# A four-layer graph network on one core: the hand-ordered slots of the attention layer replaced by a greedy assignment of tiles and steps to engines

## The chip, the cores and the metric

The kernel runs on one core of a Trainium2 chip. The core has a matrix engine (TensorE, PE), three engines for elementwise work (VectorE or DVE, ScalarE or ACT, GpSimd or POOL) and queues for transfers (here SyncE or SP issues most of them). Each engine executes its own instructions in program order and waits on semaphores for the others. Results of PE land in PSUM, of which the kernel uses eight banks of 128 x 512 float32; GpSimd works on SBUF alone in this kernel, the others on both. The metric is the device time of one execution in microseconds.

## The reference

Input x has 64 batches of 256 nodes with 128 features, and there is one 256 x 256 adjacency matrix. Four layers follow, each behind a layer norm with a ReLU and with a residual sum. All is float32. Cut to what matters:

```python
# layer 0: five steps of a gated graph network (both matrices are adj)
m = einsum('nm,bmd->bnd', adj, h);  av = concat([m, m])
z = sigmoid(av @ w3.T + w3_b + h @ u3.T + u3_b)
r = sigmoid(av @ w4.T + w4_b + h @ u3.T + u3_b)
hv = tanh(av @ w5.T + w5_b + (r * h) @ u5.T + u5_b)
h = (1 - z) * h + z * hv
# layer 1: Chebyshev hops with adj, a product with Theta1, bias, ReLU
# layer 2: (adj @ h + h) @ weight + bias, each row scaled to norm 1
# layer 3: attention over pairs of nodes (i, j), with 256 features e
pre = s1[:, :, None, :] + s2[:, None, :, :] + b_lin   # s1, s2: products of h and adj
hh  = where(pre >= 0, pre, 0.2 * pre)
e   = einsum('bije,e->bij', hh, a) + adj
out = sigmoid(einsum('bij,bjf->bif', softmax(e, axis=2), h))
x   = x + out
```

The costly part is layer 3: for each batch, 256 x 256 pairs of nodes times 256 features go through a leaky ReLU and a weighted sum over the features.

## The kernel before

**Pairs, slots and tiles.** Two batches are handled together, which makes 32 pairs. The leaky ReLU is split into a linear part, which is one projection with `g2` into the score bank, and 0.8 times a ReLU. The ReLU part is built tile by tile: a tile is 128 features x (4 rows i, 2 batches, 256 nodes j), 128 x 2048 values. A pair has 64 slots, numbered n over the whole kernel, with 4 rows i in each, and each slot has two tiles, k = 0 and k = 1, for the two halves of the 256 features. So there are 2048 slots and 4096 tiles. `scores` (L637 to L650) multiplies each tile with a window of the weight vector (`win`), four matmuls side by side, which add into the score bank of its block. A block is 32 slots, half a pair; the two score banks are used in turn.

**Who makes tiles.** `make` (L611 to L635) lets DVE make the k = 0 tile of each slot with one tensor_tensor, max(s2a, -s1 - b), from the PSUM bank `s2a`, which holds s2 of this pair and is written by one projection at the first slot of the pair (`"t_2a" not in ops`). The part that this leaves out of the ReLU is linear in i alone and cancels in the softmax over j. For k = 1 there are two kinds: in two slots of three (kind "g") GpSimd adds s1 and s2 in `make_sum` (L602 to L608, seven slots ahead) and ACT applies the ReLU to the whole tile in place (L625); in the third (kind "s") ACT makes the tile alone with eight activations of 256 values, with s1 as the bias and s2 read from a PSUM bank `s2p` (L635). Each kind has its own buffers: five for k = 0, six and two for k = 1, thirteen in all.

**Fronts and tails.** What comes before the scores of a pair p (layers 0 to 2 and the projections of layer 3) is a generator `front(p)`; its last act is to put its operands into `READY[p]`. What comes after a block (softmax, the product with h3, output) is `tail(p, ic, ...)`. A generator yields, before each step, the engine of this step, the time from which it can run, and whether it needs a spare PSUM bank; four of the eight banks are spare. A step is one to a few instructions. `norm`, `copied`, `project_token`, `to_feature` and others are helpers of these generators; where a helper issues an instruction, its line stands in the profile (L259 is that of all side-by-side matmuls but the scores).

**Order.** The program order is written while the kernel is traced. The code keeps a clock for each engine (`ran`, with a price for each step and a delay `SEEN` until others see it), and `in_order` pins each engine's instructions in the order of tracing. Fronts 0 and 1 are begun first, and front 0 is completed before the first slot. Then for each slot n: `background(n)` advances fronts and tails whose step can run by the clocks, or that are behind a due time; then the sum of slot n + 7, the tiles of slot n + 4, and the scores of slot n are issued. Front p + 2 begins when pair p's first slot comes, so two fronts are under way at once, each over about two pairs.

Of the kernel before, what the change touches and what calls it, by code (L numbers as in the profile page):

```python
# [21 lines left out]
AHEAD = 4  # L22
SUM_AHEAD = 7
# [4 lines left out]
def kernel(  # L28
# [50 lines left out]

# [12 lines left out]
    s2a, s2p = (b.rearrange("p (b n) -> p b n", b=NB) for b in banks[:2])  # L92
    pes = banks[2:4]
# [3 lines left out]
    SEEN = {PE: 0.25, DVE: 0.14, ACT: 0.15, POOL: 0.13}  # L97

    def ran(engine, us, *after):
        clock[engine] = max(clock[engine], 0.0, *after) + us  # L100
        return clock[engine] + SEEN[engine]

    spare = [[b, 0.0] for b in banks[4:]]
# [6 lines left out]
    def by_feature(b):  # L110
        return b.rearrange("p (b n) -> p b n", b=NB)
# [123 lines left out]
    nc.vector.memset(win, 0.0)  # L235
    a_rep = const.tile([P, NE, P], F32, name="a_rep")
    nc.vector.memset(a_rep, 1.0)
    nblin = const.tile([P, NE], F32, name="nblin")
    nc.vector.tensor_scalar(nblin, blin, -1.0, None, op0=OP.mult)
    for k in range(NE):  # L240
        nc.vector.tensor_scalar(win[:, k, 31:32], acol[:, k:k + 1], 1.0 - ALPHA, None, op0=OP.mult)
        nc.vector.tensor_scalar(a_rep[:, k, :], a_rep[:, k, :], acol[:, k:k + 1], None, op0=OP.mult)
# [46 lines left out]
    def project_token(pp, pairs):  # L289

        pp = by_token(pp)
        for b in range(NB):
            for c in range(NC):
                for k, (t, w) in enumerate(pairs):
                    nc.tensor.matmul(pp[:, b, c, :], t[:, b, c * P:(c + 1) * P], w,  # L295
                                     start=(k == 0), stop=(k == len(pairs) - 1))
# [13 lines left out]
    PROJECT, MIX, TURN, PRODUCT, PRODUCTS = 0.86, 1.74, 0.69, 1.18, 2.99  # L310
    COPY, BIASED, TANH, ELEMENTS = 0.48, 0.58, 0.57, 0.61

    def norm(src, since, h):
# [9 lines left out]
        t = ran(DVE, 1.04, since)  # L323
        yield POOL, t
        inverse_root(mv[:, :, 1], OP.add, LN_EPS)
        nc.gpsimd.tensor_scalar(mv[:, :, 0], mv[:, :, 0], -1.0, None, op0=OP.mult)
        nc.gpsimd.tensor_mul(mv[:, :, 0], mv[:, :, 0], mv[:, :, 1])  # L327
        t = ran(POOL, 1.6, t)
# [13 lines left out]
    KEPT = {"hT": dict(bufs=4), "hT3": {}, "s2b": {}}  # L342
# [3 lines left out]
    def front(p):  # L346
# [144 lines left out]
        yield DVE, t  # L491
# [15 lines left out]
        hT, t_hT = copied("hT3", b, t)  # L507
        yield PE, t_hT, 1
        b = take()
        project(b[0], adj_t[:, 1, P:2 * P], hT)  # L510
        t = ran(PE, PROJECT, t_hT, b[1])
        yield ACT, t
        s2b, t_2 = copied("s2b", b, t)
# [14 lines left out]
        s1n = feat("s1n")  # L528
        nc.scalar.activation(s1n, by_feature(b[0]), AF.Identity, bias=nblin[:, 0:1], scale=-1.0)
        t_n = ran(ACT, BIASED, t)  # L530
        spare.append([b[0], t_n])
        READY[p] = dict(x3=x3, h3=h3, hT=hT, s1n=s1n, s1b=s1b, s2b=s2b, t_b=max(t_b, t_2), t_n=t_n)

    def tail(p, ic, pe, since, x3, h3):
# [27 lines left out]
        for k in range(NB):  # L562
            for c in range(NC):
                nc.tensor.matmul(po[:, k, :], wT[:, k, c, :], h3[:, k, c, :], start=(c == 0), stop=(c == NC - 1))  # L564
# [19 lines left out]
    TILES = {}  # L584
    t_pe = {}
    t_free = {"v": [0.0] * 5, "g": [0.0] * 6, "s": [0.0] * 2}
# [5 lines left out]
    def kind(n):  # L592
        return "s" if n % 3 == 0 else "g"

    def operands(n, s1, s2):

        _, ic, r = where(n)
        i0 = ic * P + r
        whole = [P, 4, NB, N]
        rows = s1[:, :, i0:i0 + 97:32].rearrange("p b g -> p g b").unsqueeze(3)  # L600
        return s2.unsqueeze(1).to_broadcast(whole), rows.to_broadcast(whole)

    def make_sum(n):
        if n >= NPAIR * SLOTS or kind(n) != "g":
            return
        ops = READY[where(n)[0]]
        tile_ = relu_pool.tile([P, 4, NB, N], F32, name="rl_g", bufs=6)
        nc.gpsimd.tensor_add(tile_, *operands(n, ops["s1b"], ops["s2b"]))  # L608
        TILES[n, 1] = tile_, ran(POOL, 3.58, ops["t_b"], t_free["g"].pop(0))

    def make(n):  # L611
        if n >= NPAIR * SLOTS:
            return
        p, ic, r = where(n)
        ops = READY[p]
        if "t_2a" not in ops:
            project(banks[0], adj_t[:, 1, 0:P], ops["hT"])
            ops["t_2a"] = ran(PE, PROJECT, clock[DVE] + SEEN[DVE])
        tile_ = relu_pool.tile([P, 4, NB, N], F32, name="rl_v", bufs=5)
        nc.vector.tensor_tensor(tile_, *operands(n, ops["s1n"], s2a), op=OP.max)  # L620
        TILES[n, 0] = tile_, ran(DVE, 2.2, ops["t_2a"], ops["t_n"], t_free["v"].pop(0))
        if kind(n) == "g":
            tile_, since = TILES[n, 1]
            t = tile_.rearrange("p g b n -> p (g b n)")
            nc.scalar.activation(t, t, AF.Relu)  # L625
            TILES[n, 1] = tile_, ran(ACT, 1.8, since)
        else:
            if "t_2p" not in ops:
                nc.scalar.copy(s2p, ops["s2b"])
                ops["t_2p"] = ran(ACT, COPY, ops["t_b"])  # L630
            tile_ = relu_pool.tile([P, 4, NB, N], F32, name="rl_s", bufs=2)
            for g in range(4):
                for b in range(NB):
                    i = ic * P + g * 32 + r
                    nc.scalar.activation(tile_[:, g, b, :], s2p[:, b, :], AF.Relu,  # L635
                                         bias=ops["s1b"][:, b, i:i + 1], scale=1.0)
            TILES[n, 1] = tile_, ran(ACT, 2.86, t_free["s"].pop(0))  # L637

    def scores(n):
        p, ic, r = where(n)  # L640
        pe = pes[ic % 2]
        if r == 0:
            project(pe, g2, READY[p]["hT"], stop=False)
            ran(PE, PROJECT, t_pe.get(p * NC + ic - 2, 0.0))
        for k in range(NE):
            tile_, since = TILES.pop((n, k))

            for g in range(4):
                nc.tensor.matmul(pe[g * 32:(g + 1) * 32, :], win[:, k, 31 - r:63 - r], flat(tile_[:, g]),  # L649
                                 start=False, stop=(r == 31 and k == NE - 1), skip_group_check=True)  # L650
            t_free["v" if k == 0 else kind(n)].append(ran(PE, PROJECT, since))

    CHAINS = {}

# [3 lines left out]
    def begin_front(p):  # L658
        if p < NPAIR:
            load_x(p + 1)  # L660
            begin(p, front(p))

    def wait_of(key):

        engine, since, *bank = CHAINS[key][1]
        if bank:
            if not spare:
                return 1e9
            since = max(since, min(b[1] for b in spare))
        return since - clock[engine]  # L670

    def advance(key):
        chain = CHAINS[key]
        chain[1] = next(chain[0], None)
        chain[2] += 1
        if chain[1] is None:
            del CHAINS[key]
        return chain[2]

    in_order()  # L680
    for e in clock:
        clock[e] = 0.0
    begin_front(0)
    begin_front(1)
    total = 0
    while 0 in CHAINS:

        q = 1 if 1 in CHAINS and wait_of(1) < wait_of(0) - 1.0 else 0
        taken = advance(q)
        total = taken if q == 0 else total  # L690
        in_order()

    def background(n):
        p, k = n // SLOTS, n % SLOTS + 1
        room = SLOTS - SUM_AHEAD - 3
        while True:
            todo = []
            for key in CHAINS:
                if isinstance(key, tuple):
                    late = 2.0  # L700
                else:

                    due = total * (0.5 * (min(1.0, k / room) + 1) if key == p + 1 else 0.5 * k / SLOTS)
                    late = due - CHAINS[key][2]
                todo.append((-late, key))
            for late, key in sorted(todo, key=lambda x: x[0]):
                late = -late
                if late < -AHEAD_STEPS:
                    continue
                wait = wait_of(key)  # L710
                if wait <= TOLERANCE or late > LATE and wait < 100 or key == p + 1 and k >= room:
                    break
            else:
                return
            advance(key)

    AHEAD_STEPS, TOLERANCE, LATE = 15, 0.05, 8

    for n in range(SUM_AHEAD):
        make_sum(n)  # L720
    for n in range(AHEAD):
        make(n)
    in_order()
    for n in range(NPAIR * SLOTS):
        if n % SLOTS == 0:
            begin_front(n // SLOTS + 2)
        background(n)
        make_sum(n + SUM_AHEAD)
        make(n + AHEAD)
        scores(n)  # L730
        in_order()
        if n % 32 == 31:
            p, ic, _ = where(n)
            begin((p, ic), tail(p, ic, pes[ic % 2], clock[PE] + SEEN[PE], READY[p]["x3"], READY[p]["h3"]))
    while CHAINS:
        advance(min(CHAINS, key=wait_of))
# [31 lines left out]
```

## Time and profile before

| What | Value |
|---|---|
| Runs | 5560.47, 5561.85, 5564.78 us; median 5561.85 |
| The profiled execution's own time | 5561.99 us |
| Its span, first to last instruction | 5560.2 us |
| Mean granted TensorE clock | 0.989 |
| First DVE tile | at 146.87 us |
| HBM traffic | 9.70 MB read, 8.39 MB written, 3 GB/s over the span |

The time of a run and the span differ by 1.8 us, which lie outside the first and last instruction. Busy time is the union of an engine's instructions; instructions that overlap on one engine have durations whose sum is larger than the busy time, so what an instruction occupies is better read from the distance between two starts. Idle time is put down to what ended it. The transfers are small beside the span and stay out of the following.

### The profile page before, as it was taken

How to read it: one execution, taken by the hardware profiler on the slowest of the kernel's cores; microseconds unless marked ns; L12 is line 12 of the kernel's file. 1: busy time of each engine (PE TensorE's matmuls, PEld its weight loads, DVE VectorE, ACT ScalarE, POOL GpSimd, SP SyncE). 2: the span in 40 equal slices, each digit the busy share in tenths (PEclk: the TensorE clock that was granted, in tenths of full speed). 3: DMA queues.
4: the chain of work that ended last, by engine and by line, in shares of the span. 5: the costliest groups of instructions: out<-in, count | busy, mean ns of one | idle time of the engine just before them, and what ended most of it. 6: DMA issues, size and time to landing. Idle time of an engine off the chain costs nothing.

```text
span 5560.2 us, 122022 instructions
## 1 busy us (share of the span) xinstructions
PE 5364.9 (96%) x51733; PEld 1876.4 (34%) x51733; DVE 5273.8 (95%) x4224; ACT 5390.2 (97%) x8910; POOL 5222.9 (94%) x2075
## 2 busy tenths in 40 slices
PE   7999999999999999999999999999999999999998
PEld 3333333333333333333333333333333333333322
DVE  3989999999999999999999999999999999999998
ACT  3999999999999999999999999999999999999998
POOL 1999999999999999999999999999999999999998
PEclk9999999999999999999999999999999999999999
DMA  0000000000000000000000000000000000000000
GB/s 20 2 4 5 5 2 5 5 4 5 4 3 5 4 5 5 2 5 5 4 5 4 3 5 4 5 5 2 5 5 4 5 4 3 5 2 3 3 2 4
DMA packets 38741, 25.91 MB, mean 5 GB/s; under 512 B 3504, under 2 KB 38192, under 8 KB 38192
## 3 DMA queue, kind: packets, MB, share of 16 engines
q1 hardware_dynamic: 35088, 17.05, 1.0%
q8 instruction: 404, 6.62, 0.5%
q10 hardware_dynamic: 3104, 1.05, 0.1%
q14 instruction: 145, 1.19, 0.1%
HBM read 9.70 MB, written 8.39 MB: 3 GB/s over the span
## 4 chain that ended last, share of the span: by engine, by line
PE 56%; DVE 20%; ACT 16%; issue 6%; POOL 2%; DMA 0%; ACTq 0%; DVEq 0%; POOLq 0%; SPq 0%
PE bank L649 35%; DVE rl_v L620 16%; PE bank L259 16%; ACT rl_g L625 7%; ACT rl_s L635 6%; POOL rl_g L608 2%; PE bank L295 2%; PE bank L287 2%; PE bank L564 1%; ACT h L331 1%; DVE bank L404 1%; PE bank L280 1%; DVE d L400 1%; DVE hT L408 1%; DVE stats L320 0%
## 5 line engine op out<-in xcount | busy, mean ns | idle before, releaser
L608 POOL TENSOR_TENSOR rl_g<-s2b,s1b 128x2048 f32<-128x2048 f32 x1365 | 4901.1, 3626 | 147.6 <-PE bank L649 133.5
L620 DVE TENSOR_TENSOR rl_v<-bank,s1n 128x2048 f32<-128x2048 f32 x2048 | 4576.9, 2280 | 151.9 <-PE bank L649 89.8
L625 ACT ACTIVATE rl_g<-rl_g 128x2048 f32<-128x2048 f32 x1365 | 2846.3, 2198 | 19.0 <-POOL rl_g L608 18.7
L635 ACT ACTIVATE rl_s<-bank,s1b 128x256 f32<-128x256 f32 x5464 | 2226.4, 730 | 41.2 <-PE bank L649 40.1
L649 PE MATMUL bank<-rl_v,win 128*32 128x512 f32 x16384 | 2187.9, 599 | 12.0 <-DVE rl_v L620 11.6
L649 PE MATMUL bank<-rl_g,win 128*32 128x512 f32 x10920 | 1434.4, 595 | 14.3 <-ACT rl_g L625 14.3
L649 PEld LDWEIGHTS bank<-rl_v,win 128*32 128x32 f32 x16384 | 514.1, 110 | 1068.2 <-issue 933.2
L649 PE MATMUL bank<-rl_s,win 128*32 128x512 f32 x5464 | 754.5, 595 | 0.5 <-ACT rl_s L635 0.5
L649 PEld LDWEIGHTS bank<-rl_g,win 128*32 128x32 f32 x10920 | 352.5, 111 | 858.4 <-issue 710.6
L649 PEld LDWEIGHTS bank<-rl_s,win 128*32 128x32 f32 x5464 | 190.2, 110 | 439.5 <-issue 374.2
L259 PE MATMUL bank<-adj_t,h 128*32 128x256 f32 x5120 | 309.5, 382 | 7.4 <-ACT h L419 7.4
L259 PE MATMUL bank<-hT,adj_t 128*32 128x512 f32 x1024 | 149.0, 662 | 105.4 <-DVE rl_v L620 104.6
L259 PEld LDWEIGHTS bank<-adj_t,h 128*32 128x32 f32 x5120 | 156.2, 110 | 156.0 <-ACT h L419 34.8
L331 ACT ACTIVATE h<-x,mv 128x128 f32<-128x128 f32 x384 | 166.5, 581 | 11.8 <-POOL mv L327 11.7
L259 PE MATMUL bank<-mT,w 128*32 128x512 f32 x1280 | 168.3, 592 | 0.0
L259 PE MATMUL bank<-mT,w5t 128*32 128x512 f32 x1280 | 168.3, 592 | 0.0
L259 PE MATMUL bank<-rh,u5t 128*32 128x512 f32 x1280 | 168.2, 592 | 0.0
L395 ACT ACTIVATE bank<-bank,gate_b 128x512 f32<-128x512 f32 x160 | 156.5, 978 | 11.6 <-PE bank L259 11.2
L259 PE MATMUL bank<-hT,u3t 128*32 128x512 f32 x1280 | 166.7, 593 | 0.0
L259 PE MATMUL bank<-mT,w4t 128*32 128x512 f32 x1280 | 166.7, 592 | 0.0
L377 ACT ACTIVATE bank<-bank,gate_b 128x512 f32<-128x512 f32 x160 | 152.1, 951 | 13.2 <-PE bank L259 13.0
L381 DVE SCALAR_TENSOR_TENSOR rh<-bank,hT 128x512 f32<-128x512 f32 x160 | 109.3, 683 | 56.7 <-ACT bank L377 55.7
(111 smaller groups left out, 3458.7 us busy)
## 6 DMA issues: line engine op xcount, KB each, us to landing
xin<-in_x_dram SPq DMA_DIRECT2D x64, 128.0 KB, 2.2
out_dram<-o SPq DMA_DIRECT2D x64, 128.0 KB, 1.8
w_raw<-in_L_gnn_w_w_dram ACTq DMA_DIRECT2D x3, 128.0 KB, 2.6
th_raw<-in_L_gnn_Theta_dram ACTq DMA_DIRECT2D x1, 320.0 KB, 3.3
adj_n<-in_adj_dram SPq DMA_DIRECT2D x1, 256.0 KB, 5.0
w_raw<-in_L_gnn_u_w_dram ACTq DMA_DIRECT2D x2, 64.0 KB, 2.2
bias<-in_L_gnn_bias_dram ACTq DMA_DIRECT2D x2, 64.0 KB, 3.4
w<-in_L_gnn_weight_dram ACTq DMA_DIRECT2D x1, 64.0 KB, 3.0
```

Source lines behind the costliest of these rows:

```text
L259: nc.tensor.matmul(o[g:g + 32], w[:, g:g + 32], t, start=start, stop=stop, skip_group_check=True)
L287: nc.tensor.transpose(pt[:, b, c, :], ht[:, b, c * P:(c + 1) * P], ident)
L295: nc.tensor.matmul(pp[:, b, c, :], t[:, b, c * P:(c + 1) * P], w, start=(k == 0), stop=(k == len(pairs) - 1))
L331: nc.scalar.activation(h[:, k, :], s[:, k, :], AF.Relu, bias=mv[:, k, 0:1], scale=mv[:, k, 1:2])
L377: nc.scalar.activation(r[0], pr[0], AF.Tanh, bias=br, scale=0.5)
L381: nc.vector.scalar_tensor_tensor(rh, by_feature(r[0]), 1.0, hT, op0=OP.add, op1=OP.mult)
L395: nc.scalar.activation(pv[0], pv[0], AF.Tanh, bias=bh, scale=1.0)
L608: nc.gpsimd.tensor_add(tile_, *operands(n, ops["s1b"], ops["s2b"]))
L620: nc.vector.tensor_tensor(tile_, *operands(n, ops["s1n"], s2a), op=OP.max)
L625: nc.scalar.activation(t, t, AF.Relu)
L635: nc.scalar.activation(tile_[:, g, b, :], s2p[:, b, :], AF.Relu, bias=ops["s1b"][:, b, i:i + 1], scale=1.0)
L649: nc.tensor.matmul(pe[g * 32:(g + 1) * 32, :], win[:, k, 31 - r:63 - r], flat(tile_[:, g]), start=False, stop=(r == 31 and k == NE - 1), s ...
```

## The change

The slots are gone as an order. Names and code that change:

- Each engine takes work for itself. The main loop picks the engine whose simulated time is lowest; of the work that is ready for it (tail steps first, then front steps, then a tile) it issues one item, else it moves that engine's time on.
- DVE takes the k = 0 tiles in order, one instruction each; ACT and GpSimd share the k = 1 tiles, each taking the next when it comes free. ACT makes a tile in two parts of four activations, GpSimd in four parts of two `tensor_scalar` instructions of 256 values with a per-partition scalar. The pass of ACT over GpSimd's sums is gone.
- Signs: s2 is projected negated (`w2n`), DVE and GpSimd take the minimum and not the maximum, and their tiles meet the negated window `win_n`; ACT uses scale = -1.0.
- The thirteen tile buffers are one set; an engine holds at most 8 (DVE), 3 (ACT) or 2 (GpSimd) that are not yet scored.
- PE scores whichever tile was ready first; a block's end is counted with `left`.
- The bank of s2 for DVE is doubled (`s2v`, by the parity of the pair) and is written by a step of the front. Score banks and `s2p` move on by one, and three banks are spare in place of four.
- A front begins when `2 + scored // 128` exceeds the number begun; its steps are held back by a due time. A step of the front (x3) waits until the tail of the pair two before it has been issued.
- `project_token` and the product in `tail` use four column groups (`side_by_side`) in place of one 128-wide matmul.
- In `norm` the sign change of the mean moves from GpSimd to DVE. Prices in the planner change too.

The diff, cut to its core:

```diff
-    s2a, s2p = (b.rearrange("p (b n) -> p b n", b=NB) for b in banks[:2])
-    pes = banks[2:4]
+    s2v = banks[:2]
+    s2p = banks[2].rearrange("p (b n) -> p b n", b=NB)
+    pes = banks[3:5]
-    SEEN = {PE: 0.25, DVE: 0.14, ACT: 0.15, POOL: 0.13}
+    SEEN = {PE: 0.25, DVE: 0.14, ACT: 0.45, POOL: 0.13}
-    spare = [[b, 0.0] for b in banks[4:]]
+    spare = [[b, 0.0] for b in banks[5:]]
...
-                    nc.tensor.matmul(pp[:, b, c, :], t[:, b, c * P:(c + 1) * P], w,
-                                     start=(k == 0), stop=(k == len(pairs) - 1))
+                    side_by_side(pp[:, b, c, :], t[:, b, c * P:(c + 1) * P], w, k == 0, k == len(pairs) - 1)
...
-    PROJECT, MIX, TURN, PRODUCT, PRODUCTS = 0.86, 1.74, 0.69, 1.18, 2.99
+    PROJECT, MIX, TURN, PRODUCT, PRODUCTS = 0.86, 1.74, 0.69, 0.88, 2.64
...
+        nc.vector.tensor_scalar(mv[:, :, 0], mv[:, :, 0], -1.0, None, op0=OP.mult)
...
-        nc.gpsimd.tensor_scalar(mv[:, :, 0], mv[:, :, 0], -1.0, None, op0=OP.mult)
...
-        yield DVE, t
+        yield DVE, t, 0, lambda: p < 2 or (p - 2, NC - 1) in TAILED
         x3 = tok("x3")
...
+        s2a = s2v[p % 2]
+        yield PE, max(t_hT, t_s2v[p % 2])
+        project(s2a, w2n[:, 0:P], hT)
+        t_s2a = ran(PE, PROJECT, t_hT, t_s2v[p % 2])
...
+    tiles = [[relu_pool.tile([P, 4, NB, N], F32, name=f"rl{k}", bufs=1), 0.0] for k in range(13)]
+    MOST = {DVE: 8, ACT: 3, POOL: 2}
...
+    def tile_ready(e):
+        if e in begun:
+            return 0.0
+        n = following[e != DVE]
+        if n >= NSLOT or n // SLOTS not in READY or held[e] == MOST[e] or not tiles:
+            return None
+        return max(READY[n // SLOTS]["since"][e != DVE], min(t[1] for t in tiles))
...
+    def work_on_tile(e):
...
+        if e == DVE:
...
+            nc.vector.tensor_tensor(t, rows.to_broadcast(whole), ops["s2a"].unsqueeze(1).to_broadcast(whole), op=OP.min)
+            done = ran(DVE, 2.2, since)
...
+        elif e == ACT:
...
+            for g in (2 * part, 2 * part + 1):
+                for b in range(NB):
+                    i = i0 + g * 32
+                    nc.scalar.activation(t[:, g, b, :], s2p[:, b, :], AF.Relu, bias=ops["s1"][1][:, b, i:i + 1], scale=-1.0)
+            done = ran(ACT, 1.43, since)
         else:
...
+            for b in range(NB):
+                i = i0 + part * 32
+                nc.gpsimd.tensor_scalar(t[:, part, b, :], ops["s2n"][:, b, :], ops["s1"][1][:, b, i:i + 1], None, op0=OP.min)
+            done = ran(POOL, 1.8, since)
...
+    def score_ready():
+        best = None
+        for tile_ in made:
...
+            if block not in left:
+                if block >= 2 and block - 2 not in t_pe:
+                    continue
+                since = max(since, t_pe.get(block - 2, 0.0))
+            if best is None or since < best[0]:
+                best = since, tile_
+        return best
...
+    STEPS_OF_FRONT, SPREAD, AHEAD = 106, 1.8, 8
...
+    def chain_ready(key, e):
...
+        if not isinstance(key, tuple) and key > 0:
+            due = STEPS_OF_FRONT * (scored[0] / (2 * SLOTS) - (key - 2)) / SPREAD
+            if CHAINS[key][2] > due + AHEAD:
+                return None
+        return max(since, min(b[1] for b in spare)) if bank else since
...
+    while scored[0] < 2 * NSLOT or CHAINS:
+        while begun_fronts[0] < NPAIR and begun_fronts[0] < 2 + scored[0] // (2 * SLOTS):
+            begin_front()
+        e = min(now, key=now.get)
...
+        ready = [x for x in todo if x[0] <= now[e] + 0.05]
+        if ready:
+            _, (rank, *_), what = min(ready, key=lambda x: x[1])
+            if rank < 2:
+                advance(what)
+            elif e == PE:
+                score(what)
             else:
+                work_on_tile(e)
```

## The prediction, made before the changed kernel ran

> **What bounds the kernel now.** I read the page's first two parts, then busy time by stretch, then the waits and groups, and last the timeline for what one instruction really occupies.
>
> ```profile
> PE 5364.9 (96%) x51733; PEld 1876.4 (34%) x51733; DVE 5273.8 (95%) x4224; ACT 5390.2 (97%) x8910; POOL 5222.9 (94%) x2075
> ...
> DVE  3989999999999999999999999999999999999998
> ```
>
> Four engines are over 94% busy, so none alone can be called the bound. The leading 3 of DVE is the prologue: the first tile starts at 146.87 us. Then the stretches:
>
> ```profile
> 2000.00:2169.00 169.00, 164.42 (x1608) 57.53 (x1604) 163.76 (x132) 168.07 (x280) 162.90 (x65) 0.99 0.02 5
> 2169.00:2338.00 169.00, 165.74 (x1616) 58.20 (x1612) 163.94 (x132) 167.36 (x277) 162.49 (x66) 0.99 0.02 4
> ```
>
> The columns are PE, PEld, DVE, ACT, POOL. One pair of batches takes about 169 us. The starts of the copy on L629, which comes once per pair, are 146.40 us for pair 0 and 5397.87 us for pair 31: 5251.5 / 31 = 169.4 us a pair. The periods go 167, 167, 174.5 and again. DVE has 164.2 us of work in it; ACT is busy for nearly all of it. Where the rest goes:
>
> ```profile
> POOL rl_g L608 <- PE bank L649: 133.5, 71, 4.5
> ...
> PE bank L259 <- DVE rl_v L620: 104.6, 31, 4.5
> ...
> DVE rl_v L620 <- PE bank L649: 89.8, 87, 2.6
> ...
> DVE rl_v L620 <- PE bank L259: 59.1, 31, 10.9
> ```
>
> (total us, times, longest.) The lines with 31 are the pair boundaries: PE stands 3.4 us before the product into s2a because DVE still reads the old one, and DVE then waits 1.9 us for that product. The L649 lines are makers that wait for a tile buffer.
>
> ```profile
> L608 POOL TENSOR_TENSOR rl_g<-s2b,s1b 128x2048 f32<-128x2048 f32 x1365 | 4901.1, 3626 | 147.6 <-PE bank L649 133.5
> L620 DVE TENSOR_TENSOR rl_v<-bank,s1n 128x2048 f32<-128x2048 f32 x2048 | 4576.9, 2280 | 151.9 <-PE bank L649 89.8
> L625 ACT ACTIVATE rl_g<-rl_g 128x2048 f32<-128x2048 f32 x1365 | 2846.3, 2198 | 19.0 <-POOL rl_g L608 18.7
> L635 ACT ACTIVATE rl_s<-bank,s1b 128x256 f32<-128x256 f32 x5464 | 2226.4, 730 | 41.2 <-PE bank L649 40.1
> ```
>
> These durations overlap, so the timeline gives the occupancy:
>
> ```profile
> 2004.47 3.68 ACT L635 ACTIVATE rl_s<-bank,s1b 128x256 f32<-128x256 f32 x8
> 2007.32 2.63 ACT L625 ACTIVATE rl_g<-rl_g 128x2048 f32<-128x2048 f32 x1
> 2009.12 1.38 ACT L392 ACTIVATE bank<-bank,gate_b 128x512 f32<-128x512 f32 x1
> ```
>
> Start to start, eight short activations take 2.85 us, one Relu pass 1.80, a tanh 0.57. The same reading gives 2.20 us for a DVE tile and 0.86 for a tile on PE.
>
> **What the Trainium skill says.** "TensorEngine Tiling (Array Packing)", Key Properties: a change of tiling mode drains the TensorE. The trace agrees: the 128-wide product on L295 starts 0.11 us late between 32-wide ones and holds PE for 1.20 us where its eight matmuls are 0.11 apart. "TensorE: Matmul & The Clock Gate", "Wait — 56ns, not 53.3ns?": start to start is never under about 25 ns; here 32 matmuls of 256 columns take 1.73 us, 54 ns each, so 128 columns would come at 27, just above. "GPSIMD Engine Reference", Engine selection: two-input operations pay for a shared read port, one-input ones run near line rate. The trace: 738 ns for a two-input 128x256 (L578), 408 for a one-input (L577). "SBUF — State Buffer", Who interferes with whom: a DVE instruction with at most one SBUF input leaves GpSimd alone; the DVE tile reads one operand from PSUM before and after. No run here tests that.
>
> **The change, part by part.**
>
> DVE: still makes all 2048 tiles of k = 0, min in place of max, 64 x 2.20 = 141 us a pair, plus the same steps. The sign change in norm comes over from POOL: 4 x 0.08 = 0.3 us a pair. 164.2 + 0.3 = 164.5. This is the new floor, since DVE is given no k = 1 tile.
>
> ACT and POOL: the 1365 Relu passes (1365 x 1.80 = 2457 us) go, and both engines now make whole k = 1 tiles. ACT's other work is 31 us a pair (5390 - 2457 - 683 x 2.85 = 986 us, / 32). An ACT tile costs 2.85. A POOL tile is eight tensor_scalar with a per-partition scalar, 128x256, which the trace doesn't show. From below: 8 x 0.49 (L577 with its gap) = 3.9 us. From above: like the two-input L578 with a gap, 8 x 0.83 = 6.6, or the planner's 8 x 0.90 = 7.2 in the diff. The planner's other prices agree with the trace within 0.1 us a step, so I take 7.2. Then at 167 us a pair ACT can make (167 - 31) / 2.85 = 48 tiles and POOL (167 - 9) / 7.2 = 22: 70 for the 64 needed. 6 tiles of slack; both fall behind DVE as limits. If one instruction really takes over 0.955 us, the 21 tiles that the plan puts there take 21 x 7.64 + 9 = 169.5 us and POOL gives all back.
>
> PE: the same tiles. From spacings, a pair is 159 units of 0.86 (tiles, projections), 8 node mixes of 1.73, 10 transposes of 0.69 and the 128-wide products (3.0 + 1.2 + 2 x 1.2): 136.7 + 13.8 + 6.9 + 6.6 = 164.0. The products in four column groups at 27 ns cost 2.64 + 3 x 0.88 = 5.3: 1.3 us less, 162.7. If 54 ns were a floor for them they would cost 10.4 and PE 167.8.
>
> s2 in two banks: the boundary waits (3.4 us of PE, 1.9 of DVE a pair) go. Price: three spare banks in place of four. A front holds two (pr and r or pv), a tail one: enough for one front at a time. Tiles in any order, 13 shared buffers: PE no longer stands behind a late tile, and the 174.5 us periods, which come from the n % 3 pattern, go too.
>
> Fronts: before, two fronts run at once, each over two pairs. Now front q begins when 128 (q - 1) tiles are scored, so it has about one pair's time to become READY. Its latency is the new question. In the prologue front 0 takes from its first stats at 23.98 us to 146.87: 122.9 us, front 1 beside it. Adding its steps by the spacings gives 118, so 119 alone. Under load each step that comes from another engine waits for the rest of a tile piece: DVE 19 steps x 0.86 busy x 1.1 = 18 us, and three norms that come 0.14 us after a DVE step and so behind a whole tile, 3 x 2.06 less their share, +3; ACT 33 x 0.76 x 0.71 = 18; PE 32 x 0.64 x 0.43 = 9; POOL 5 x 0.9 x 0.9 = 4. Together 52 us, less 1 for the sign change: L = 170 us.
>
> **The sum.** With L above a pair's work W, front q + 1 begins when pair q - 1 is used up, which is before READY[q]: the stall is g = L - P and the period P = (L + W) / 2. W = 164.5 + 1 to fill PE = 165.5. In the stall the chain runs unhindered, so L = 170 - 0.3 g. This gives g = 2.0, P = 167.5. Time = 146.9 prologue (the two first fronts as before) + 31 x 167.5 + 157 for the last pair (no front left: 64 x 2.2 + 4 of tails, then 11 us from last score to end as now) + 1.8 outside the span = 5498 us. Against the profiled run's 5561.99 (span 5560.2) and the median of the runs, 5561.85, 1.1% less. I take 5495.
>
> **The rivals.**
> 1. The front fits into the pair (L under 165): DVE never stalls, P = 165.5, time 5436. For it: the k = 1 makers may run ahead of DVE, which brings `scored` and so the next front forward. Against: my waits add up to more. Chance 0.20.
> 2. The front is late: one chain with about 105 hand-overs on loaded engines replaces two overlapping ones. Where the waits are 70 us and not 52, L = 187, g = 9.5, P = 175, time 5730. It decides from L = 174, where P = 169.5 as now. For it: three spare banks, and DVE tiles slip in wherever a step is ready 0.14 us later. Against: steps go ahead of tiles on every engine. Chance 0.20.
> 3. POOL's instruction is dearer than 0.955 us: at 1.05, 21 x 8.4 + 9 = 185 us a pair, about 6050. Against: both measured neighbours are under 0.83. Chance 0.08.
> 4. Nothing much is left: engines at 98% in a fixed order slip on small differences between plan and chip, or small matmuls cost PE 54 ns: P = 168.5 to 170, 5530 to 5576. For it: two periods in three are already 167. Chance 0.10.
>
> **Numbers.** My forecast, 5460 to 5540, has 0.42; the rivals as above. The range 5420 to 5650 leaves out rival 3, the far half of 2 and little else. What this kernel's measurement can tell from no change is about 0.2%, 11 us. Faster: 0.40 + 0.20 + 0.04 = 0.64; same 0.06; slower 0.30.
>
> **What would show it.** The L259 boundary waits gone from the waits; no Relu over whole tiles, about 43 ACT tiles and 21 POOL tiles a pair; DVE 97 to 98% busy from 150 us on; one DVE idle of about 2 us a pair, ended by ACT's s1a or the s2 copy (rival 2: over 6 us a pair there; rival 1: none). POOL's tensor_scalar near 0.9 us; over 0.955 with PE waiting for POOL is rival 3. L295 and L564 in fours 0.11 us apart. I am wrong in the mechanism if DVE's idle is behind PE or POOL and not at READY.

## The result, and the profile after

| | Before | After |
|---|---|---|
| Median of four runs | 5561.84 us (5560.47 to 5564.78) | 5522.43 us (5521.90 to 5525.01) |
| Span of the profiled execution | 5560.2 us | 5520.6 us |

The ratio is 0.9929, with a 95% interval from 0.9912 to 0.9947: the changed kernel is 0.7% faster. The forecast was 5495 us, 1.2% faster, in a range from 5420 to 5650.

First lines of parts 1 and 2 of the changed kernel's page. Then the busy time by stretch (PE, PEld, DVE, ACT, POOL, each with its number of instructions, then clock and DMA): one stretch in the kernel before, then the same in the changed one.

```profile
PE 5376.7 (97%) x56341; PEld 1942.7 (35%) x56341; DVE 5314.8 (96%) x4355; ACT 5012.2 (91%) x13193; POOL 5038.5 (91%) x5854
...
ACT  3998899989989998999899899989998999999898
```

```profile
1000.00:2000.00 1000.00, 978.51 (x9592) 344.41 (x9588) 971.61 (x778) 991.50 (x1646) 962.49 (x385) 0.99 0.02 5
```

```profile
1000.00:2000.00 1000.00, 984.18 (x10444) 351.48 (x10440) 981.75 (x803) 924.43 (x2438) 934.79 (x1086) 1.00 0.02 5
```

ACT went from 991 us in 1000 to 924 and POOL from 962 to 935; DVE rose from 972 to 982 and PE from 979 to 984. So ACT and POOL have slack now, and DVE and PE are nearly full. Which of the two bounds the kernel, if either does, these shares don't tell. The costly groups of the page show that the makers do what the diff says:

```profile
L647 POOL TENSOR_SCALAR rl<-s2n,s1b 128x256 f32<-128x256 f32 x5272 | 4741.5, 937 | 103.5 <-PE bank L685 51.8
L628 DVE TENSOR_TENSOR rl<-s1a,bank 128x2048 f32<-128x2048 f32 x2048 | 4552.1, 2278 | 39.6 <-ACT s1a L534 39.6
L641 ACT ACTIVATE rl<-bank,s1b 128x256 f32<-128x256 f32 x11112 | 4436.2, 978 | 1.0
```

No Relu over whole tiles is left. GpSimd makes 5272 / 8 = 659 tiles (20.6 a pair), ACT 11112 / 8 = 1389 (43.4 a pair). A GpSimd tile costs 4741.5 / 659 = 7.19 us.

What DVE waits for, over the whole span (total us, times, longest):

```profile
DVE d L400 <- ACT bank L395: 50.1, 31, 5.1
DVE rl L628 <- ACT s1a L534: 39.6, 21, 10.3
DVE rs L573 <- ACT sc L552: 29.9, 11, 2.9
DVE rh L381 <- ACT bank L377: 21.5, 24, 9.9
```

The waits of DVE's tiles for L259 (now L260) and for buffers behind L649 (now L685) are gone from this list. In their place stands the wait of a tile for `s1a`, the last thing that a front makes. Most of `d` and `rh` falls into the first 400 us, as the same list from 400 to 5200 us shows:

```profile
DVE rs L573 <- ACT sc L552: 28.8, 10, 2.9
DVE rl L628 <- ACT s1a L534: 26.5, 19, 2.8
DVE d L400 <- ACT bank L395: 8.0, 18, 0.5
DVE rh L381 <- ACT bank L377: 6.0, 19, 0.5
```

Two pair boundaries of DVE's timeline show what the first two lines are:

```profile
2148.45 4.47 DVE L628 TENSOR_TENSOR rl<-s1a,bank 128x2048 f32<-128x2048 f32 x2
2152.84 0.86 DVE L320 BATCH_NORM_STATS2 stats<-xin 128x6 f32<-128x128 f32 x4
...
2154.91 0.69 DVE L547 TENSOR_REDUCE nmx<-sc 128x2 f32<-128x512 f32 x1
2158.47 0.17 DVE L573 RECIPROCAL rs<-sums 128x2 f32<-128x2 f32 x1 [2.87 <-ACT sc L552]
2161.40 6.68 DVE L628 TENSOR_TENSOR rl<-s1a,bank 128x2048 f32<-128x2048 f32 x3 [2.76 <-ACT s1a L534]
...
2310.31 17.66 DVE L628 TENSOR_TENSOR rl<-s1a,bank 128x2048 f32<-128x2048 f32 x8
2327.90 0.68 DVE L543 TENSOR_TENSOR sc<-bank,adj_n 128x512 f32<-128x512 f32 x1
```

At 2152.84 the tiles of one pair have run out. Until 2161.40 DVE has only some steps, and it idles 2.87 + 2.76 = 5.6 us, although the first of these idles carries the name of another step. ACT's timeline has `s1a` at that moment, and the columns at its end say that ACT was waiting for PE's projection:

```profile
2160.68 0.69 ACT L534 ACTIVATE s1a<-bank,blin 128x512 f32<-128x512 f32 x1 [0.23 <-PE bank L260]
```

At the next boundary tiles run through from 2310.31 to 2327.97, with no gap. At the one after that DVE idles for 0.2 us, and then the pattern begins again. The starts of `s1a` come every 163.1, 170.8 and 172.6 us and again; from 468.63 us (pair 2) to 5362.71 (pair 31) the mean is 4894.08 / 29 = 168.8 us, against 169.4 before. The first statistics of a front come right behind the used-up pair, and from there to its `s1a` are 165.4 us (809.73 to 975.10), 174.7 (972.97 to 1147.69) and 171.0 (1139.85 to 1310.83), and so on in this pattern: 170.4 on average. So a front takes about as long as a pair, and now and then DVE stands waiting for it. That this is what keeps the gain small is the reading which the experiments test.

### The profile page after: what moved, and what is told of

It is laid out like the page before. It is cut to its first block, busy times and chain, and to the rows that moved or that the text cites. A ratio compares the mean times of both kernels' runs of the same rounds, so it can differ in the third digit from the quotient of the medians.

```text
span 5520.6 us, 138813 instructions
## 1 busy us (share of the span) xinstructions
PE 5376.7 (97%) x56341; PEld 1942.7 (35%) x56341; DVE 5314.8 (96%) x4355; ACT 5012.2 (91%) x13193; POOL 5038.5 (91%) x5854
## 4 chain that ended last, share of the span: by engine, by line
PE 46%; DVE 28%; ACT 22%; issue 3%; POOL 1%; DMA 0%; ACTq 0%; POOLq 0%; SPq 0%; DVEq 0%
PE bank L685 29%; DVE rl L628 22%; ACT rl L641 17%; PE bank L260 15%; PE bank L288 1%; ACT bank L395 1%; DVE stats L320 1%; DVE bank L404 1%; ACT h L331 1%; DVE hT L408 1%; ACT bank L377 1%; DVE d L400 1%; ACT h L419 1%; PE bank L281 1%; ACT sc L552 1%
## 5 line engine op out<-in xcount | busy, mean ns | idle before, releaser
L647 POOL TENSOR_SCALAR rl<-s2n,s1b 128x256 f32<-128x256 f32 x5272 | 4741.5, 937 | 103.5 <-PE bank L685 51.8
L628 DVE TENSOR_TENSOR rl<-s1a,bank 128x2048 f32<-128x2048 f32 x2048 | 4552.1, 2278 | 39.6 <-ACT s1a L534 39.6
L641 ACT ACTIVATE rl<-bank,s1b 128x256 f32<-128x256 f32 x11112 | 4436.2, 978 | 1.0
L685 PE MATMUL bank<-rl,win_n 128*32 128x512 f32 x21656 | 2785.3, 594 | 29.7 <-DVE rl L628 28.4
L685 PE MATMUL bank<-rl,win 128*32 128x512 f32 x11112 | 1598.2, 594 | 0.0
L685 PEld LDWEIGHTS bank<-rl,win_n 128*32 128x32 f32 x21656 | 734.4, 110 | 1487.9 <-issue 1196.7
L685 PEld LDWEIGHTS bank<-rl,win 128*32 128x32 f32 x11112 | 397.0, 110 | 766.7 <-issue 567.0
L260 PE MATMUL bank<-adj_t,h 128*32 128x256 f32 x5120 | 318.1, 382 | 17.0 <-ACT h L419 16.4
L260 PEld LDWEIGHTS bank<-adj_t,h 128*32 128x32 f32 x5120 | 166.5, 110 | 199.1 <-ACT h L419 89.5
L377 ACT ACTIVATE bank<-bank,gate_b 128x512 f32<-128x512 f32 x160 | 172.7, 1079 | 58.8 <-issue 29.1
L392 ACT ACTIVATE bank<-bank,gate_b 128x512 f32<-128x512 f32 x160 | 176.7, 1105 | 8.9 <-PE bank L260 8.9
L395 ACT ACTIVATE bank<-bank,gate_b 128x512 f32<-128x512 f32 x160 | 170.9, 1068 | 14.3 <-PE bank L260 14.3
L337 ACT COPY mT<-bank 128x512 f32<-128x512 f32 x160 | 165.6, 1035 | 15.7 <-PE bank L260 15.6
L260 PE MATMUL bank<-hT,u3t 128*32 128x512 f32 x1280 | 175.3, 594 | 0.0
L260 PE MATMUL bank<-mT,w4t 128*32 128x512 f32 x1280 | 174.6, 594 | 0.0
L260 PE MATMUL bank<-mT,w 128*32 128x512 f32 x1280 | 174.1, 592 | 0.0
L260 PE MATMUL bank<-rh,u5t 128*32 128x512 f32 x1280 | 174.0, 592 | 0.0
L260 PE MATMUL bank<-mT,w5t 128*32 128x512 f32 x1280 | 174.0, 592 | 0.0
L419 ACT COPY h<-bank 128x512 f32<-128x512 f32 x128 | 149.1, 1165 | 5.1 <-PE bank L288 5.1
```

Source lines behind the costliest of these rows:

```text
L260: nc.tensor.matmul(o[g:g + 32], w[:, g:g + 32], t, start=start, stop=stop, skip_group_check=True)
L337: nc.scalar.copy(c, by_feature(bank[0]))
L377: nc.scalar.activation(r[0], pr[0], AF.Tanh, bias=br, scale=0.5)
L392: nc.scalar.activation(pr[0], pr[0], AF.Tanh, bias=bz, scale=0.5)
L395: nc.scalar.activation(pv[0], pv[0], AF.Tanh, bias=bh, scale=1.0)
L419: nc.scalar.copy(h, by_token(b[0]))
```

## The experiments

Each ratio is to the kernel before, measured beside the run on the same chip (5562.9 to 5566.3 us there, 5561.8 beside the changed kernel). So a difference between a run and the changed kernel's 5522.43 us is uncertain by some 4 us. The names: theory F is that of the front's latency, P = (L + W) / 2 for a period P (from one pair to the next), a latency L (from a front's first statistics to its `s1a`) and a pair's work W on DVE; D says that DVE's work is the bound, E that PE's is.

### Fronts begun earlier

```diff
-        while begun_fronts[0] < NPAIR and begun_fronts[0] < 2 + scored[0] // (2 * SLOTS):
+        while begun_fronts[0] < NPAIR and begun_fronts[0] < 2 + (scored[0] + SLOTS) // (2 * SLOTS):
```

> Each front begins 64 tiles, half a pair, earlier than in the changed kernel; nothing else is touched. Theory F (the front's latency of 165 to 175 us against a pair's work sets the period, P = (L + W) / 2): a front that has half a pair more is READY in time, the stall before s1a goes, and the period falls from 168.8 us to DVE's own work plus small waits, 166 to 167.5: 5430 to 5480 us. Rival D (DVE, 98% busy, is the bound and its idle is slip between plan and chip) and rival E (PE, 96% full by its spacings, is the bound): the period stays, 5505 to 5535 us.

5437.53 us, ratio 0.9769 [0.9753, 0.9786]: 85 us less than the changed kernel, by one added term, as F said. D and E, under which nothing should have changed, don't hold for the changed kernel. The same stretch of this run, and the next:

```profile
1000.00:2000.00 1000.00, 989.94 (x10612) 351.08 (x10608) 996.48 (x804) 944.98 (x2492) 955.53 (x1112) 1.00 0.02 5
2000.00:3000.00 1000.00, 990.09 (x10655) 352.45 (x10651) 996.59 (x822) 943.78 (x2489) 950.91 (x1109) 1.00 0.02 5
```

DVE is 99.65% busy, and its wait list between 2000 and 5190 us is empty, where the changed kernel has 44 us. The starts of `s1a` come every 165.6 us (1083.74 to 2574.13, nine periods). Two fronts are under way at once for a part of the time, and each takes longer: 194.1 us from 392.05 to 586.15. They are ready in time all the same. No kernel of the study is faster.

### Fronts begun later

```diff
+        while begun_fronts[0] < NPAIR and begun_fronts[0] < 2 + max(0, scored[0] - 8) // (2 * SLOTS):
```

> Each front begins 8 tiles, about 10 us, later than in the changed kernel. Theory F: the front of pair q + 1 now begins after READY of pair q, so the period is its latency plus this delay, 12 + 170 us less what the idle engines save: 175 to 180 us, 5720 to 5880 us. Rivals D and E: a chain that is ready some us later in a schedule that has other work changes nothing: under 5550 us.

5813.21 us, ratio 1.0444 [1.0429, 1.0460], with periods of 179.4, 178.5 and 178.0 us, as F said. Of its DVE waits:

```profile
DVE rl L628 <- ACT s1a L534: 332.3, 31, 11.7
```

The wait comes once for every pair boundary, 10.7 us each. Ten microseconds of a single chain's start cost 290 us, 9.4 a pair: at the boundary DVE has no other tile to make. A front takes a little less here than in the changed kernel: 166.3, 167.7 and 166.8 us (845.54 to 1011.79, 1023.51 to 1191.22, 1202.94 to 1369.69).

### Inner norms that follow at once

Behind x1, x2 and x3 the time handed to `norm` is DVE's own clock, without the 0.14 us until others see the result. One of the three places:

```diff
         t = ran(DVE, ELEMENTS, t)
         spare.append([b[0], t])
+        t = clock[DVE]
```

> The statistics of the three inner norms may follow the DVE step before them at once, where in the changed kernel they are ready 0.14 us later and stand behind a whole tile of 2.20 us. No instruction is added or taken away. Theory F: L falls by 3 x 2.06 = 6 us, the period by up to 3 us: 5430 to 5490 us. Rivals D and E: the engines' work is the same, 5505 to 5535 us.

5459.27 us, ratio 0.9810 [0.9796, 0.9825]. No instruction less, and 63 us are gone, as F said. From the first statistics to `s1a` it is now 162.4 and 164.8 us (1133.70 to 1296.11, 1303.39 to 1468.23), 170.4 before: 6.8 us less, for 6 that were expected. By the formula such fronts are in time and the period should be 165.6 us; it is 166.6 (467.94 to 5298.71, 29 periods), and this last 1.0 is not explained.

### The 128-wide products back

`project_token` and the product in `tail` as in the kernel before, with their old prices.

> The products of layers 1, 2 and 3 go back to one 128-wide matmul each, as in the kernel before, and their prices in the plan too. PE gets 1.3 us a pair more work. Rival E: every us on PE is a us of the period, 5522 + 32 x 1.3 = 5565 us. Theory F: only the two products of the front lengthen L, by 0.65 us, half of which counts: 5525 to 5545 us. Rival D: 5520 us. If the matmuls of 128 columns in four groups had a floor of 54 ns, this kernel would be faster than the changed one, by up to 3 us a pair, 5430 us.

5542.89 us, ratio 0.9960 [0.9945, 0.9974]: 20 us more than the changed kernel, whose interval it just touches. That is in F's range and half of E's. But it is not the 0.65 us of F's sum: the fronts take 172.9 and 174.7 us by turns (1987.15 to 2160.09, 2160.15 to 2334.89), 3.4 more than in the changed kernel. With this L the formula gives 169.7 us, and 169.8 are measured (462.70 to 5385.95, 29 periods). Why the fronts grew by more than their products is not shown. The four-group products cost what was taken for them. PE's timeline of the changed kernel has the product of a tail with what follows, 0.88 us from start to start:

```profile
2086.68 1.06 PE L260 MATMUL bank<-h,wT 128*32 128x128 f32 x32
2087.56 1.04 PE L685 MATMUL bank<-rl,win_n 128*32 128x512 f32 x8
```

### One bank of s2 in the changed kernel

```diff
-    s2v = banks[:2]
+    s2v = [banks[0], banks[0]]
...
-    spare = [[b, 0.0] for b in banks[5:]]
+    spare = [[b, 0.0] for b in banks[5:] + banks[1:2]]
...
-        yield PE, max(t_hT, t_s2v[p % 2])
+        yield PE, max(t_hT, t_s2v[0]), 0, lambda: following[0] >= p * SLOTS
...
```

> The changed kernel with one bank of s2 for DVE, as before the change, and so four spare banks; the front's step that writes it waits until DVE has been given its last tile of the pair before. Theory F: the last eight steps of the front, about 6 us, always come after DVE's last tile, so every pair boundary has them as a stall where now one in three has: the period grows by 1 to 4 us, 5560 to 5650 us. If the fourth spare bank were worth more than the second s2 bank, under 5520 us.

5631.10 us, ratio 1.0116 [1.0101, 1.0131]: 109 us more than the changed kernel, although a fourth bank is spare. As expected, the end of the front cannot begin before DVE's last tile, at every boundary. PE waits for that tile, and DVE then for what PE and ACT make:

```profile
PE bank L260 <- DVE rl L628: 73.0, 31, 3.4
```

```profile
DVE sc L543 <- PE bank L685: 125.4, 32, 7.3
DVE rl L628 <- ACT s1a L534: 59.8, 32, 10.2
```

From 400 to 5100 us DVE idles 4.5 to 6.8 us at each boundary, 5.5 on average. The period is 172.4 us, 3.6 more than in the changed kernel, whose boundaries have 1.9 on average.

### Two banks of s2 in the kernel before

```diff
-    s2a, s2p = (b.rearrange("p (b n) -> p b n", b=NB) for b in banks[:2])
-    pes = banks[2:4]
+    s2v = banks[:2]
+    s2p = banks[2].rearrange("p (b n) -> p b n", b=NB)
+    pes = banks[3:5]
...
+        if n % SLOTS == 0:
+            project(s2v[p % 2], adj_t[:, 1, 0:P], ops["hT"])
+            ops["t_2a"] = ran(PE, PROJECT)
...
```

> The kernel before with only the two banks of s2 added (three spare banks, the projection issued with the first sum of the pair, seven slots ahead); slots, kinds and overlapping fronts stay. If the boundary waits of the kernel before (3.4 us of PE and 1.9 us of DVE a pair) were on its path, the period falls from 169.4 by 1.5 to 3 us: 5470 to 5520 us, which is as much as the whole change gave. If they were hidden, or the fourth spare bank counts as much: 5550 us and over.

5558.52 us, ratio 0.9985 [0.9979, 0.9992]: 8 us less than the kernel before. The wait is gone and the time is not. First a line of DVE's list in the kernel before, then the list in this kernel (L654 is L649 of before, where 59.1 us were for L259 and 89.8 for L649):

```profile
DVE d L400 <- ACT bank L395: 12.0, 10, 1.8
```

```profile
DVE rl_v L625 <- PE bank L654: 112.3, 95, 3.9
DVE d L401 <- ACT bank L396: 46.9, 28, 6.7
...
DVE rl_v L625 <- PE bank L260: 9.7, 1, 9.7
```

The 49 us that the boundary no longer takes come back as waits for buffers (+22.5) and for ACT's tanh (`d`: +34.9), with 9 less at `rh`. From the first DVE tile of pair 2 to that of pair 30 the mean period is 169.1 us, against 169.6 before. This kernel also has one spare bank less than the kernel before; what that costs is not separated.

### PE relieved

In the kernel with early fronts PE leaves out the scores of 4 of the 64 k = 0 tiles of a pair, in the kernel and in the plan, so these are missing from the sum.

```diff
-        for g in range(4):
+        for g in range(4 if k or n % 16 != 15 or left[block] == 0 else 0):
```

> The kernel with fronts begun early, in which PE leaves out the scores of the k = 0 tiles of 4 slots in 64; DVE still makes these tiles. PE has 3.4 us a pair less work. If PE is the bound of that kernel: 3.4 x 31 = 105 us less than its 5437, 5330 us. If DVE is (99.7% busy there), the same time within 0.4%, 5415 to 5445 us.

5440.00 us, ratio 0.9773 [0.9757, 0.9790], the same as with all scores. PE, which is busy for 99% of a stretch of that kernel, is not what bounds it. That leaves DVE, at 99.65%.

### Early fronts and following norms together

> Fronts begun half a pair earlier and the inner norms following at once, both edits together. Theory F: with fronts that are READY in time a shorter front buys nothing more: 5425 to 5445 us, that of the early fronts alone. If the norm edit acted through something else than the front's latency (fewer waits on any engine), the two gains add: 5437 - 63 = 5375 us.

5442.00 us, ratio 0.9777 [0.9762, 0.9791]: no gain over the early fronts alone. Where the fronts are in time a shorter front is worth nothing, so what the norm edit gave by itself came through the front's latency.

### Scores in the order of the slots

On the kernel with early fronts:

```diff
-            if best is None or since < best[0]:
+            if 2 * tile_[1] + tile_[2] == scored[0] and (best is None or since < best[0]):
                 best = since, tile_
```

> The kernel with fronts begun half a pair earlier, in which PE scores the tiles strictly in the order of the slots (n, k = 0 before k = 1) as the kernel before does; makers take tiles as they come free. Theory G (with the fronts in time, most of the gain over the kernel before comes from PE not standing behind a late tile, a GpSimd tile takes 7.2 us): 5500 to 5570 us. Rival H (it comes from ACT's freed Relu passes, and the order of scoring is covered by the buffers): under 5460 us.

5487.27 us, ratio 0.9859 [0.9844, 0.9874]. Between the two expectations, so neither held. The order costs 50 us of the 128 between the kernel before and this kernel with free order. PE waits for GpSimd now, which it did for 0.5 us with free order, and DVE waits for tile buffers, which it did not there:

```profile
PE bank L685 <- POOL rl L647: 61.4, 70, 2.5
```

```profile
DVE rl L628 <- PE bank L685: 37.4, 48, 2.5
```

The second line is nearly all of what the profiled execution has lost, 40.5 us (a span of 5476.7 for 5436.2). This fits one chain: while PE waits for a late tile, the tiles behind it keep their buffers, and DVE has none to write to.

### How much earlier is enough

The edit is that of the early fronts, with 4 and with 12 tiles in place of 64.

> The changed kernel with each front begun 4 tiles, about 5.3 us, earlier. Theory F: P = (L + W - 5.3) / 2 while the front is still late, so up to 2.6 us a pair less and not below what fronts in time give: 5440 to 5490 us. If the gain of the early fronts came from two fronts overlapping for half a pair, almost nothing: 5505 us or more.

> The changed kernel with each front begun 12 tiles, about 16 us, earlier. Theory F: 16 us is more than the stall at any boundary, so the whole gain of the fronts begun 64 tiles earlier: 5430 to 5445 us. If overlap of two fronts is what counts: 5470 us or more.

With 12 tiles: 5444.21 us, 0.9789 [0.9773, 0.9805], as F said. The rival, that two fronts must overlap for half a pair, wanted 5470 or more here and falls. With 4 tiles: 5507.11 us, 0.9898 [0.9883, 0.9913], too little a gain for F's formula and just inside the rival's range. The starts of `s1a` tell why. From pair 3 to 14 they come every 167.1 us on average (623.44 to 2461.17, eleven periods). Then the order of the plan tips into another pattern: 182 and 158.6 by turns, 169.3 on average (2641.31 to 4503.45). DVE's timeline at the tipping point:

```profile
2625.88 6.67 DVE L628 TENSOR_TENSOR rl<-s1a,bank 128x2048 f32<-128x2048 f32 x3
2638.63 0.69 DVE L381 SCALAR_TENSOR_TENSOR rh<-bank,hT 128x512 f32<-128x512 f32 x1 [6.07 <-ACT bank L377]
2640.53 0.69 DVE L543 TENSOR_TENSOR sc<-bank,adj_n 128x512 f32<-128x512 f32 x1 [1.21 <-PE bank L685]
...
2642.03 4.48 DVE L628 TENSOR_TENSOR rl<-s1a,bank 128x2048 f32<-128x2048 f32 x2
```

No tile from 2632.55 to 2642.03: the same starved boundary, with its idle time under the names of `rh` and `sc`. So the late front is still the cause. What failed is a fixed L and the same stall at every boundary: in the second pattern the fronts take 181.0 and 177.0 us (2801.20 to 2982.15, 2963.74 to 3140.76). With 179.0 the formula, less 5.3 / 2, gives 169.6. Before that they take 171 us on average (pairs 3 to 14), and the formula gives 165.7 where 167.1 are measured.

## Why the prediction came out as it did

**The mechanism was right.** The front's latency replaced the old waits, and it was the limit in the case held likeliest. DVE's idle time is where it was said to be: 55 of the 70 us in its list from 400 to 5200 us are the two waits at the boundary. The stall g was put at 2.0 us a pair; boundaries of 5.6, 0 and 0.2 us make 1.9. The average was foreseen, the pattern was not. W was put at 165.5; the kernel whose fronts are in time has 165.6. Rival 1's time for that case, 5436 us, is what the early fronts then gave, 5437.53. Shifting only the start of the front, in either direction, or only its length, moved the time as this says; taking PE's work away did not.

**L was near in part by luck.** It was put at 170 us, 169.4 with what the stall takes off (0.3 g), and measured as 170.4. But it is not a constant of the kernel. The wide products, 0.65 us of the front's own steps, lengthened it by 3.4 us, and with a start four tiles earlier it is 177 and 181 us in the run's second pattern. A sum of average waits, as the prediction has it, can't foresee that.

**The period was mis-sized by 1.3 us:** 168.8 for 167.5. From L = 170.4 and W = 165.6 the formula P = (L + W) / 2 gives 168.0; half a microsecond of the error is thus L. That a stall shortens the chain may still be right: with stalls of 10.7 us the late fronts took 166 to 168. The remaining 0.8 is not explained; small waits of DVE for ACT (`d` and `rh`, 14 us from 400 to 5200 us, 0.5 a pair) are a part of it at most. 29 such periods, 1.3 us each, make 37 us. Against this, the first two pairs took 323.7 us (144.91 to 468.63) and not 335, 11 us less: front 2 begins only behind pair 0, so pair 0 had no more to carry than the rest of front 1 (`s1a` at 244.98). The ends of the sum, 147 and 157 us, were 144.9 and 157.9. Together 5520.6 for 5498 less 1.8.

**Single costs.** GpSimd's tile was taken at 7.2 us, the upper bound, against 3.9 from the nearest row: 7.19. The planner's price was right, and so was the reason for trusting it, that its other prices agreed; the trace of before has no such instruction. The statement of the Trainium skill that one-input operations run near line rate ("GPSIMD Engine Reference", Engine selection) is not borne out, if an operation with a per-partition scalar counts as one of these: 937 ns for 256 values, 3.7 ns each. Rival 3's threshold of 0.955 us an instruction was 6% away (0.899 by busy time). The sign change on DVE was put at 0.08 us, 0.3 a pair. Its group on L323 has 0.27 us each by duration; from its start to that of the next instruction it is 0.08 in the median and 0.14 on average, 0.6 a pair. The four-group products were right. The rule that the prediction takes from "SBUF — State Buffer", Who interferes with whom, holds there only outside DVE's 2-port perf modes (modes that use a second pair of ports, shared with GpSimd), which the prediction leaves out. By the same section a `tensor_tensor`, as the DVE tile is, has no such mode. The trace agrees: the 10 tile instructions of GpSimd that fell into idle time of DVE after 400 us took 938 ns on average, and those beside a busy DVE took 938 too.

**What the prediction had wrong** is what the waits of before were worth. It let the 3.4 us of PE and 1.9 us of DVE at a pair boundary go as a part of the gain. In the kernel before, the second bank, for one spare bank less, gave 8 us in all, since DVE then waited for buffers and for ACT. In the changed kernel the same exchange is worth 109 us, because there it keeps the last steps of the front out of the boundary.

It also misread the periods of before. No pair takes 174.5 us. The copy on L629, by which they were taken, stands before the pair's first slot with n % 3 = 0. As 64 leaves 1 when divided by 3, that is slot 0, 2 or 1 of the pair by turns, and from copy to copy are 66, 63 or 63 slots. The first DVE tiles of the pairs show the real periods: from pair 3 to pair 30 they come every 168.2 to 170.5 us. Those of pairs 10, 11 and 12 in the kernel before, which carry the wait of the boundary, stand 170.2 and 168.8 us apart:

```profile
1841.31 2.29 DVE L620 TENSOR_TENSOR rl_v<-bank,s1n 128x2048 f32<-128x2048 f32 x1 [1.19 <-PE bank L259]
2011.54 2.29 DVE L620 TENSOR_TENSOR rl_v<-bank,s1n 128x2048 f32<-128x2048 f32 x1 [2.06 <-PE bank L259]
2180.33 2.29 DVE L620 TENSOR_TENSOR rl_v<-bank,s1n 128x2048 f32<-128x2048 f32 x1 [1.19 <-PE bank L259]
```

So there were no long periods for the change to remove, and rival 4 had no periods of 167 us to lean on. The mean of 169.4, which the sum uses, is right.

**Where the expected gain went.** With fronts in time the change is worth 2.3%, 128 us (5565.37 and 5437.53 side by side). The changed kernel has 39 of these, so the late front gives some 88 back. About 50 of the 128 come from the free order of scoring, by the run that took it away. How the rest is shared between ACT's freed passes, the shared buffers and the products was not taken apart, except for the products (20 us in the changed kernel).

## What to carry to other kernels

When a schedule nearly fills every engine, look for the longest chain of single hand-overs and compare its latency under load with the time it is given. A first estimate of that latency is the steps, plus half of what each engine is busy with at each hand-over; here it moved from 164 to 194 us with the schedule, so measure it in the trace. A chain that starts one period ahead and takes a little more than a pair's work bounds the kernel though no engine is full. Starting it 12 tiles earlier cost nothing here. Before a wait is priced as a gain, ask what the waiting engine would wait for next: a removed wait that comes back under another name is no gain. And before a period is read off a marker, ask whether the marker stands at the same place in every period.

## What had not been expected of the hardware

A `tensor_scalar` on GpSimd over 128x256 takes 937 ns with a per-partition scalar from a tile (0.90 us from start to start), and 408 ns with two immediates (L577 before). The former is dearer than the two-input addition of the same shape, 738 ns (L578 before). What of this is due to the scalar's place and what to the operation (a minimum here, a product and a sum there) was not separated.
